# Diagonals of B written into zeros in DRAM and read back, in a four-layer selective-scan network

## The chip, the cores and the metric

The kernel runs on one core of a Trainium2 chip. A core has a matrix engine (TensorE, PE in the profile, its weight loads PEld), a vector engine (VectorE, DVE), an engine for activation functions and copies (ScalarE, ACT), a general engine (GpSimd, POOL) and a small one that here only issues DMA requests (SyncE, SP). Sixteen DMA engines move the data between DRAM and the on-chip memory. All arithmetic is in fp32. The metric is the time of one execution on the device, in microseconds (us); less is better. Times of single instructions come from one profiled execution.

## The reference

The input x has the shape 4 x 64 x 64 x 128. Layers 0, 1 and 3 are vision state-space blocks, layer 2 is a gated block that costs far less. A state-space block, cut to what matters here (DI = 256 channels, N = 16 states, R = 8, K = 4 directions, L = 4096 positions):

```python
xs    = stack([x0, x1, x0[..., ::-1], x1[..., ::-1]])      # rows, columns, both backwards
x_dbl = einsum('bkdl,kcd->bkcl', xs, x_proj_w)             # 8 + 16 + 16 rows: dt, B, C
delta = softplus(einsum('bkrl,kdr->bkdl', dts, dt_w) + dt_b)
h     = exp(delta_t * A) * h + (delta_t * x_t) * B_t       # for each position t, channel d and state n
y_t   = sum over n of h * C_t
```

In front of the scan stand a layer norm, a projection and a 3 x 3 depthwise convolution with SiLU; behind it a norm, a gate, a projection back and an MLP with GELU. The recurrence runs for 4 images x 3 layers x 4 directions x 256 channels x 16 states over 4096 positions.

## The kernel before

**Tiling.** The positions of one direction are cut into 8 chunks of 512. There are 12 turns (two images taken in turns through layers 0, 1 and 3), 32 chunks per turn (4 directions x 8), 384 chunks in all. Forward directions (k = 0, 1) make up 192 chunks, backward ones (k = 2, 3) the other 192. A chunk is worked through in eight periods, `i` = 0 to 7; a period handles 4 states (`CQ`) for one half of the channels (128 partitions). So period `i` uses the state group `q = i // 2`, and each group serves two periods.

**What a period does.** ACT computes the decays `exp(delta * A)` (`decay`, L907, tile `da`). DVE runs four scans over 512 positions (L923, tile `h`). The first two take their input `delta * x * B` from a PSUM tile `dbp`, which PE fills: `pair_db` (L898) multiplies the transposed `delta * x` (`duT`) with diagonal matrices that hold B for two states, so that the product is `delta * x` scaled by position. For the last two scans ACT copies `delta * x` (`du`) to PSUM (`lift`, L915, tile `dv`) and DVE multiplies it with rows of B spread over the partitions (L1050, L1051, tile `bb`). POOL multiplies the states with the spread rows of C (`times_c`, L935, tile `cb`; L937 adds in pairs in even periods). PE adds the products up into `yp` (`add_up`, L948). `dbp` has one buffer; `bb`, `cb`, `diag` and `xd` have two, `h` and `hc` four.

**The diagonals before.** `diagonals` (L884) makes, for one half of a state group, four 128 x 128 matrices on ACT, each the identity scaled by one column of `bt` (L890). `bt` is B with positions on the partitions: four transposes on PE (L850) and a copy on ACT (L855). One call stands at the end of each period, after `lift`; the two halves of a group are made three and two periods before the first period that scans with it.

**The prologue.** The rows [dt; B; C] of the next chunk are prepared meanwhile, piece by piece. `prologue` is a generator; `piece(2 * i)` in the middle of period `i` and `piece(2 * i + 1)` at its end advance it if the number is in `PIECES`. A forward chunk computes the rows of both directions (`ps_x`, L834), copies them to `xd` on ACT (L836), and stores them in DRAM (`xd_d`, L853), from where `spread` (L871) reads B and C back as broadcasts, one `bb` of 512 KB and one `cb` of 1 MB per state group, in odd periods, one group ahead. A backward chunk reads its rows from DRAM (L829). Before, the pieces are: 0 load of `xs`; 3 `xd` load or `ps_x`; 4 copy to `xd` and the first half of the dt product (L841); 6 and 8 delta (L844, L846) and the transposes of B; 9 the store of [dt; B; C], `bt` and the first `du`; 10 to 13 the rest.

**The order.** It is written out by hand: the instructions of each engine run in the order in which the Python code emits them, and each engine waits by semaphores. All DMA requests are issued by SP in that order, so one that must wait holds back all behind it. SP waits only for what a request needs, so it often stands periods ahead of the other engines. Between the steps of a period `other` slips in side work: the norms, projections, convolution and MLP that lead from one turn to the next (lines 190 to 759, tiles `gap`, `cen`, `wide`, `hid`). One of its requests is the store `x_col_d<-down` (L472), which writes a transposed image in runs of 8 values.

```python
    scan(s, i, 0, 1, da[0], s.db[:, :, 1])
    times_c(s, i, 0)
    if before:
        add_up(*before, 0)
    if then:
        pair_db(*then)          # dbp of the next period
    piece(2 * i)
    other(1)
    if spreads:
        spread(*spreads, 1)     # cb, in odd periods
```

Of the kernel before, what the change touches and what calls it, by code (L numbers as in the profile page):

```python
# [13 lines left out]
F32 = mybir.dt.float32  # L14
AF = mybir.ActivationFunctionType
# [7 lines left out]
DI, N, R, K = 256, 16, 8, 4  # L23
NX = R + 2 * N
HID = 4 * C
CH = 512
NCH = L // CH
RPC = CH // W
P = 128
WP = W + 2  # L30

CQ = 4

PAIRED = (0, 2, 4, 6)


PIECES = (0, 3, 4, 6, 8, 9, 10, 11, 12, 13)


_VSS = [  # L40
# [58 lines left out]
def vss_stack_kernel(ctx: ExitStack, tc: tile.TileContext, x: bass.AP, weights, out: bass.AP, n_batch=B, layers=(0, 1, 2, 3)):  # L99
# [6 lines left out]
    nc = tc.nc  # L106

    const = ctx.enter_context(tc.tile_pool(name="const", bufs=1))
    keep = ctx.enter_context(tc.tile_pool(name="keep", bufs=1, space=DRAM))

    ident = const.tile([P, P], F32, name="ident")
# [14 lines left out]
    for i in layers:  # L126
# [14 lines left out]
        t = const.tile([P, small_n + VSS_N - tail_at], F32, name=f"w{i}")  # L141
# [27 lines left out]
    def cols(c):  # L169
        return slice(c * CH, (c + 1) * CH)  # L170
# [13 lines left out]
    y_sb = const.tile([P, 2, L], F32, name="y_sb")  # L184
# [574 lines left out]
        return [S[a:z] for a, z in zip([0] + marks[1:], marks[1:] + [len(S)])]  # L759


    turns = []
    for e in range(0, n_batch, 2):
        for i in (0, 1, 3):
# [2 lines left out]
    for turn, (e, i) in enumerate(turns):  # L767

        for nth, k in enumerate((1, 3, 0, 2) if turn else (0, 1, 3, 2)):
            for ci in range(NCH):  # L770
                s = SimpleNamespace(turn=turn, e=e, v=wt[i], layer=i, nth=nth, k=k, ci=ci)
                s.c = NCH - 1 - ci if k >= 2 else ci
                s.columns, s.back = k % 2 == 1, k >= 2
                s.end = 0 if s.back else CH - 1
                s.step = slice(None, None, -1 if s.back else 1)
                s.first, s.last = ci == 0, ci == NCH - 1
                s.flip = len(chunks) % 2
                s.diag, s.cb, s.bb, s.h, s.hc = {}, {}, {}, {}, {}
                chunks.append(s)
    per_turn = K * NCH  # L780

# [27 lines left out]
    def scans(pool, ring, deep, psum):  # L809
# [4 lines left out]
        def prologue(s):  # L814


            lane, v = lanes[s.e % 2], s.v
            s.xs = ring.tile([P, 2, CH], F32, tag="xs", name="xs")
            nc.sync.dma_start(out=s.xs, in_=(lane.x_col if s.columns else lane.x_row)[:, :, cols(s.c)])
            if s.first:  # L820
                s.dt = pool.tile([R, DI], F32, tag="dt", name="dt_w")
                nc.sync.dma_start(out=s.dt, in_=weights[s.layer][1][:, s.k * DI : (s.k + 1) * DI])
            yield


            s.xd_d = lane.xd[s.k % 2][s.c]
            s.xd = pool.tile([2 * NX, CH], F32, tag="xd", name="xd")
            if s.back:
                nc.sync.dma_start(out=s.xd[:NX], in_=s.xd_d[1])  # L829
                yield  # L830
            else:
                ps = psum.tile([P, CH], F32, tag="misc", name="ps_x")
                for m in range(2):
                    nc.tensor.matmul(ps[: 2 * NX], v["xp"][:, s.k % 2, m, :], s.xs[:, m], start=(m == 0), stop=(m == 1))  # L834
                yield
                nc.scalar.copy(s.xd, ps[: 2 * NX])  # L836
            s.delta = pool.tile([P, 2, CH], F32, tag="delta", name="delta")
            halves = (s.flip, 1 - s.flip)
            for m in halves:
                ps = psum.tile([P, CH], F32, tag="misc", name="ps_dt")  # L840
                nc.tensor.matmul(ps, s.dt[:, m * P : (m + 1) * P], s.xd[:R], start=True, stop=True)  # L841
                yield
                func = AF.Identity if m == halves[0] else AF.Softplus
                nc.scalar.activation(s.delta[:, m], ps, func, bias=v["dtb"][:, s.k, m : m + 1])  # L844
            m = halves[0]
            nc.scalar.activation(s.delta[:, m], s.delta[:, m], AF.Softplus)  # L846
            nc.scalar.preload_act_table_set("natural_log_exp_and_others")
            ps = psum.tile([P, 4, NX], F32, tag="misc", name="ps_bt")
            for j in range(4):
                nc.tensor.transpose(ps[:, j, :], s.xd[:NX, j * P : (j + 1) * P], ident[:NX, :NX])  # L850
            yield
            if not s.back:
                nc.sync.dma_start(out=s.xd_d.rearrange("k r t -> (k r) t"), in_=s.xd)  # L853
            s.bt = pool.tile([P, 4, N], F32, tag="bt", name="bt")
            nc.scalar.copy(s.bt, ps[:, :, R : R + N])  # L855
            s.du = pool.tile([P, 2, CH], F32, tag="du", name="du")
            for m in halves:
                nc.gpsimd.tensor_mul(s.du[:, m], s.delta[:, m], s.xs[:, m])  # L858
                yield
            s.duT = pool.tile([P, 4, 2, P], F32, tag="duT", name="duT")  # L860
            for m in halves:
                ps = psum.tile([P, 4, P], F32, tag="misc", name="ps_duT")
                for j in range(4):
                    nc.tensor.transpose(ps[:, j, :], s.du[:, m, j * P : (j + 1) * P], ident)
                yield
                nc.scalar.copy(s.duT[:, :, m, :], ps)
            yield

        def spread(s, q, b):

            rows_of, at, count = ((s.bb, CQ * q + 2, CQ - 2), (s.cb, CQ * q, CQ))[b]  # L871
            rows_of[q] = pool.tile([P, count, CH], F32, tag="bc"[b] + "b", name="bc"[b] + "b")
            row = R + b * N + at
            nc.sync.dma_start(
                out=rows_of[q], in_=s.xd_d[s.k // 2 : s.k // 2 + 1, row : row + count].to_broadcast([P, count, CH])
            )
# [4 lines left out]
            q = i // 2  # L881
            return q, (i + q + s.flip) % 2

        def diagonals(s, q, half):  # L884

            if half == 0:
                s.diag[q] = pool.tile([P, 4, P, 2], F32, tag="diag", name="diag")
            for t in (2 * half, 2 * half + 1):
                for j in range(2):
                    nc.scalar.activation(  # L890
                        s.diag[q][:, t, :, j], ident, AF.Copy, scale=s.bt[:, t, CQ * q + j : CQ * q + j + 1]
                    )

        def pair_db(s, i):
            q, m = place(s, i)
# [6 lines left out]
        def decay(s, i, side):  # L902
            q, m = place(s, i)
            da = ring.tile([P, 2, CH], F32, tag="da", name="da")
            for j in range(2):
                n = CQ * q + 2 * side + j
                nc.scalar.activation(da[:, j], s.delta[:, m], AF.Exp, scale=s.v["a"][:, s.k, m, n : n + 1])  # L907
            return da
# [5 lines left out]
        def lift(s, i):  # L914
            nc.scalar.copy(dv[i % 2], s.du[:, place(s, i)[1]])  # L915
# [17 lines left out]
        def times_c(s, i, side):  # L933
            hc = s.hc[i, side] = deep.tile([P, 2, CH], F32, tag="hc", name="hc")
            nc.gpsimd.tensor_mul(hc, s.h[i, side], s.cb[i // 2][:, 2 * side : 2 * side + 2, :])  # L935
            if side == 1 and i in PAIRED:
                nc.gpsimd.tensor_add(hc, hc, s.hc[i, 0])  # L937

        def add_up(s, i, side):
            if side == 0 and i in PAIRED:  # L940
                return
            q, m = place(s, i)
            start, end = (0, 7) if m == s.flip else (1, 6)
            opens = i == start and side == int(i in PAIRED)
            if opens:
                setattr(s, f"yp{m}", psum.tile([P, CH], F32, tag=f"yp{m}", name="yp"))
            for j in range(2):
                nc.tensor.matmul(  # L948
                    getattr(s, f"yp{m}"),
                    ident,  # L950
                    s.hc[i, side][:, j],
                    start=opens and j == 0,
                    stop=i == end and side == 1 and j == 1,
                )
            if i == end and side == 1:
                full.append((s, m))
# [15 lines left out]
        for step in sum([combine(0, psums)] + opening[:4], []):  # L972
            step()
        s = chunks[0]
        pro = prologue(s)
        for _ in pro:
            pass
        for q, half in ((0, 0), (0, 1), (1, 0)):
            diagonals(s, q, half)
        spread(s, 0, 0)  # L980
        spread(s, 0, 1)
        pair_db(s, 0)
# [5 lines left out]
        for at, (s, i) in enumerate(periods):  # L988
            then = periods[at + 1] if at + 1 < len(periods) else None
            if i == 0:  # L990
                nxt = chunks[at // 8 + 1] if at // 8 + 1 < len(chunks) else None
# [14 lines left out]
            def piece(number):  # L1006

                if nxt and number in PIECES:
                    next(pro)
# [33 lines left out]
            other(1)  # L1043
            if spreads:
                spread(*spreads, 1)
            if then:
                da_next[1] = decay(*then, 1)
            save(s, i, 0)
# [6 lines left out]
            times_c(s, i, 1)  # L1055
            if then:
                lift(*then)

            q, half = (i + 2 + i % 2) // 2, 1 - i % 2
            if q < 4:  # L1060
                diagonals(s, q, half)
            elif nxt:
                diagonals(nxt, q - 4, half)
            if i < 2 and full:
                leave(*full.pop(0))
            if before:
# [108 lines left out]
```

## Time and profile before

| | |
|---|---|
| median of 3 runs | 22674.4 us (22664.0 to 22679.19) |
| the profiled execution's own time | 22684.1 us |
| its span, first to last instruction | 22682.3 us |
| granted TensorE clock, mean | 0.956 |
| busy: PE, DVE, ACT, POOL | 87%, 86%, 82%, 85% |
| DMA | 3060 MB in 2.44 million packets, 43.1% of 16 engines on SP's queue |
| first scan of turn 1, of turn 2 | 1982.3 us, 3791.2 us |

The profiled execution is 9.7 us above the median of the runs. Busy shares are shares of the span. A row of the groups reads: line, engine, operation, what is written from what, shapes and count; then busy us in total and mean ns of one; then the idle time of the engine ahead of them and what ended it. A row of the waits reads: who waited, for whom, us in total, times, and the longest. In the timeline a row has its start, its length, the engine (SPq is SP's request queue), the line and the tiles, and in brackets the idle time ahead of it. Turn 1 lasts from 1982.3 to 3791.2, 56.5 us per chunk; turn 3, which has the gated layer as its side work, from 5600.4 to 7587.3, 62.1 us per chunk.

### The profile page before, as it was taken

Reading aid. Unit: us, or ns where it says so; the run is one execution under the profiler, and the core shown is the slowest. Engines: PE = TensorE matmul, PEld = TensorE weight load, DVE = VectorE, ACT = ScalarE, POOL = GpSimd, SP = SyncE. Lnnn points to the kernel's source line nnn. Section 1 sums busy time; section 2 is a strip of 40 time slices with the busy share of each in tenths; the row PEclk is TensorE's granted clock in tenths of the full one; section 3 lists DMA queues with packets and bytes.
Section 4 is the critical chain, followed back from the end, with each engine's and each line's share of the span. In section 5 each row is a group of like instructions: output and inputs, shape, how many; then the busy total and the mean of one; then the engine's idle time right before and its main releaser. Section 6 shows DMA issues by size and latency. Waiting matters only on the chain. (4 is left out here: it accounts for less than half of the span.)

```text
span 22682.3 us, 216904 instructions
## 1 busy us (share of the span) xinstructions
PE 19815.6 (87%) x58234; PEld 10564.4 (47%) x58234; DVE 19497.9 (86%) x20186; ACT 18647.2 (82%) x40022; POOL 19246.5 (85%) x8862
## 2 busy tenths in 40 slices
PE   7888898888888888889889988888888888888887
PEld 3444444444444444444444444444444444444443
DVE  5999888988888888889889889898888888888996
ACT  5888888888887887888888888888888878888887
POOL 5999888888788878888888888888887888888996
PEclk8999999999999999999999999999999999999999
DMA  4444444444334434534534544444443453344333
GB/s 106 149 143 147 134 135 145 137 134 141 122 126 135 137 121 129 145 131 141 146 136 141 145 145 134 135 146 134 133 144 122 125 138 128 126 133 144 139 140 105
DMA packets 2437558, 3060.09 MB, mean 135 GB/s; under 512 B 1753840, under 2 KB 1790064, under 8 KB 2238192
## 3 DMA queue, kind: packets, MB, share of 16 engines
q1 hardware_dynamic: 2436336, 3046.22, 43.1%
q8 instruction: 472, 7.73, 0.1%
q14 instruction: 750, 6.14, 0.1%
HBM read 2784.41 MB, written 261.49 MB: 134 GB/s over the span
## 5 line engine op out<-in xcount | busy, mean ns | idle before, releaser
L935 POOL TENSOR_TENSOR hc<-h,cb 128x1024 f32<-128x1024 f32 x6144 | 14406.9, 2362 | 2937.3 <-DVE h L923 1825.8
L948 PE MATMUL yp<-hc,ident 128*128 128x512 f32 x18432 | 9030.4, 616 | 632.2 <-POOL hc L937 477.4
L907 ACT ACTIVATE da<-delta,w 128x512 f32<-128x512 f32 x12288 | 8149.8, 712 | 682.2 <-DVE h L923 668.0
L923 DVE TENSOR_TENSOR_SCAN h<-da,state,dbp 128x512 f32<-128x512 f32 x5376 | 6569.2, 1261 | 1123.5 <-PE dbp L898 893.0
L898 PE MATMUL dbp<-diag,duT 128*128 128x256 f32 x24576 | 6105.1, 392 | 1014.8 <-DVE h L923 965.7
L923 DVE TENSOR_TENSOR_SCAN h<-da,state,dv 128x512 f32<-128x512 f32 x5376 | 6583.5, 1263 | 0.0
L898 PEld LDWEIGHTS dbp<-diag,duT 128*128 128x128 f32 x24576 | 4720.4, 195 | 3320.5 <-issue 2038.1
L948 PEld LDWEIGHTS yp<-hc,ident 128*128 128x128 f32 x18432 | 3479.7, 196 | 4957.0 <-issue 3671.2
L890 ACT ACTIVATE diag<-ident,bt 128x128 f32<-128x128 f32 x12288 | 3951.5, 401 | 0.0
L937 POOL TENSOR_TENSOR hc<-hc 128x1024 f32<-128x1024 f32 x1536 | 3622.5, 2358 | 120.4
L915 ACT COPY dv<-du 128x512 f32<-128x512 f32 x3072 | 1800.2, 586 | 1208.3 <-DVE h L923 1202.0
L1050 DVE TENSOR_TENSOR dv<-dv,bb 128x512 f32<-128x512 f32 x3072 | 2083.0, 678 | 665.3 <-ACT dv L915 553.3
L1051 DVE TENSOR_TENSOR dv<-dv,bb 128x512 f32<-128x512 f32 x3072 | 2113.8, 688 | 0.0
L444 PE MATMUL gap<-halo,cw 128*128 128x512 f32 x3456 | 1757.2, 607 | 14.2 <-DVE cen L281 7.6
L841 PE MATMUL ps_dt<-xd,dt_w 8*128 8x512 f32 x1536 | 896.5, 664 | 287.1 <-DMA xd<-xd_d 149.8
L923 DVE TENSOR_TENSOR_SCAN h<-da,dbp 128x512 f32<-128x512 f32 x768 | 893.4, 1201 | 236.8 <-PE dbp L898 190.4
L858 POOL TENSOR_TENSOR du<-delta,xs 128x512 f32<-128x512 f32 x768 | 979.0, 1275 | 32.8 <-ACT delta L846 32.8
L931 ACT COPY state<-h 128x2 f32<-128x2 f32 x5376 | 962.1, 179 | 0.0
L444 PEld LDWEIGHTS gap<-halo,cw 128*128 128x128 f32 x3456 | 631.4, 192 | 661.9 <-issue 605.6
L923 DVE TENSOR_TENSOR_SCAN h<-da,dv 128x512 f32<-128x512 f32 x768 | 892.6, 1201 | 0.0
L844 ACT ACTIVATE delta<-ps_dt,w 128x512 f32<-128x512 f32 x768 | 524.5, 683 | 215.9 <-PE ps_dt L841 211.0
L281 DVE TENSOR_TENSOR cen<-cen,gap 128x512 f32<-128x512 f32 x256 | 175.0, 684 | 533.0 <-ACT gap L278 531.9
(122 smaller groups left out, 11908.7 us busy)
## 6 DMA issues: line engine op xcount, KB each, us to landing
cb<-xd_d SPq DMA_DIRECT2D x1536, 1024.0 KB
bb<-xd_d SPq DMA_DIRECT2D x1536, 512.0 KB
xs<-x_row_d SPq DMA_DIRECT2D x192, 512.0 KB
xs<-x_col_d SPq DMA_DIRECT2D x192, 512.0 KB
x_col_d<-down SPq DMA_DIRECT2D x192, 256.0 KB
x_row_d<-wide SPq DMA_DIRECT2D x96, 512.0 KB
y_d<-y_sb SPq DMA_DIRECT2D x96, 512.0 KB
y<-y_d SPq DMA_DIRECT2D x96, 512.0 KB
```

Of the source, the lines that this page charges most:

```text
L444: nc.tensor.matmul(z.ps, z.cw[:, m, t, :], z.halo[c][:, dy : dy + RPC, dx : dx + W], start=(t == 0), stop=(t == 8),)
L858: nc.gpsimd.tensor_mul(s.du[:, m], s.delta[:, m], s.xs[:, m])
L890: nc.scalar.activation(s.diag[q][:, t, :, j], ident, AF.Copy, scale=s.bt[:, t, CQ * q + j : CQ * q + j + 1])
L898: nc.tensor.matmul(s.db[:, t * P : (t + 1) * P, :], s.duT[:, t, m, :], s.diag[q][:, t], start=True, stop=True)
L907: nc.scalar.activation(da[:, j], s.delta[:, m], AF.Exp, scale=s.v["a"][:, s.k, m, n : n + 1])
L915: nc.scalar.copy(dv[i % 2], s.du[:, place(s, i)[1]])
L923: nc.vector.tensor_tensor_scan(s.h[i, side][:, j, s.step], da[:, j, s.step], db[:, s.step], init, ALU.mult, ALU.add)
L935: nc.gpsimd.tensor_mul(hc, s.h[i, side], s.cb[i // 2][:, 2 * side : 2 * side + 2, :])
L937: nc.gpsimd.tensor_add(hc, hc, s.hc[i, 0])
L948: nc.tensor.matmul(getattr(s, f"yp{m}"), ident, s.hc[i, side][:, j], start=opens and j == 0, stop=i == end and side == 1 and j == 1,)
L1050: nc.vector.tensor_mul(db, du, s.bb[i // 2][:, 0])
L1051: nc.vector.tensor_mul(du, du, s.bb[i // 2][:, 1])
```

## The change

The diagonals are no longer computed. Two DRAM arrays `diag_d`, one for even and one for odd chunks, are filled with zeros once at the start. Each has a part for each of the four state groups, of 512 rows of 258 values. For a chunk, two stores write 2048 single values each from `xd`: value t of B's rows for state j (0 or 1) of every group goes to place j of row t. Read with a row length of 256 instead of 258, row p of a block of 128 has these two values at 2p and 2p + 1, so a plain read of 512 KB gives the tile `diag` as `pair_db` wants it. The zeros around are never overwritten, and the values of the next chunk but one go to the same places.

The reads stand in odd periods right behind the request for C, one per odd period; the first `pair_db` that uses one is emitted two periods later. The transposes of B on PE and `bt` fall away. The store of [dt; B; C] moves from piece 9 to piece 5, with the two stores of values right behind it; the first half of the dt product moves from 4 to 5, its bias step from 6 to 7; the load of `xd` of a backward chunk moves from piece 3 to piece 0.

```diff
-PIECES = (0, 3, 4, 6, 8, 9, 10, 11, 12, 13)
+DIAG = 2 * P + 2
+PIECES = (0, 3, 4, 5, 7, 8, 9, 10, 11, 12, 13)
...
+    diag_d = []
+    zero = y_sb.rearrange("p m l -> p (m l)")[:, : N // CQ * 4 * DIAG]
+    nc.vector.memset(zero, 0.0)
+    for j in range(2):
+        diag_d.append(keep.tile([N // CQ, CH * DIAG], F32, name=f"diag_d{j}"))
+        nc.sync.dma_start(
+            out=diag_d[j].rearrange("q (p c) -> p q c", p=P), in_=zero.rearrange("p (q c) -> p q c", q=N // CQ)
+        )
...
+                s.diag_d = diag_d[s.flip]
...
-            yield
             s.xd_d = lane.xd[s.k % 2][s.c]
             s.xd = pool.tile([2 * NX, CH], F32, tag="xd", name="xd")
             if s.back:
                 nc.sync.dma_start(out=s.xd[:NX], in_=s.xd_d[1])
+            yield
+            if s.back:
                 yield
...
                 nc.scalar.copy(s.xd, ps[: 2 * NX])
+            yield
+            if not s.back:
+                nc.sync.dma_start(out=s.xd_d.rearrange("k r t -> (k r) t"), in_=s.xd)
+            rows = s.diag_d.rearrange("q (t c) -> q t c", c=DIAG)
+            for j in range(2):
+                nc.sync.dma_start(out=rows[:, :, j], in_=s.xd[R + j : R + N : CQ])
...
-            ps = psum.tile([P, 4, NX], F32, tag="misc", name="ps_bt")
-            for j in range(4):
-                nc.tensor.transpose(ps[:, j, :], s.xd[:NX, j * P : (j + 1) * P], ident[:NX, :NX])
             yield
-            if not s.back:
-                nc.sync.dma_start(out=s.xd_d.rearrange("k r t -> (k r) t"), in_=s.xd)
-            s.bt = pool.tile([P, 4, N], F32, tag="bt", name="bt")
-            nc.scalar.copy(s.bt, ps[:, :, R : R + N])
...
-        def diagonals(s, q, half):
-            if half == 0:
-                s.diag[q] = pool.tile([P, 4, P, 2], F32, tag="diag", name="diag")
-            for t in (2 * half, 2 * half + 1):
-                for j in range(2):
-                    nc.scalar.activation(
-                        s.diag[q][:, t, :, j], ident, AF.Copy, scale=s.bt[:, t, CQ * q + j : CQ * q + j + 1]
-                    )
+        def diagonals(s, q):
+            s.diag[q] = pool.tile([P, 4, P, 2], F32, tag="diag", name="diag")
+            nc.sync.dma_start(
+                out=s.diag[q].rearrange("p t c n -> p t (c n)"),
+                in_=s.diag_d[q].rearrange("(t p c) -> p t c", t=4, c=2 * P)[:P],
+            )
...
             if spreads:
                 spread(*spreads, 1)
+            if i % 2:
+                q = i // 2 + 2
+                if q < 4:
+                    diagonals(s, q)
+                elif nxt:
+                    diagonals(nxt, q - 4)
...
-            q, half = (i + 2 + i % 2) // 2, 1 - i % 2
-            if q < 4:
-                diagonals(s, q, half)
-            elif nxt:
-                diagonals(nxt, q - 4, half)
```

More of the change, by code (lines that the diff above doesn't have):

```diff
@@ L977, in scans @@
             pass
-        for q, half in ((0, 0), (0, 1), (1, 0)):
-            diagonals(s, q, half)
+        for q in range(2):
+            diagonals(s, q)
         spread(s, 0, 0)
@@ L1045, in scans @@
                 spread(*spreads, 1)
+            if i % 2:
+                q = i // 2 + 2
+                if q < 4:
+                    diagonals(s, q)
+                elif nxt:
+                    diagonals(nxt, q - 4)
             if then:
@@ L1057, in scans @@
                 lift(*then)
-            q, half = (i + 2 + i % 2) // 2, 1 - i % 2
-            if q < 4:
-                diagonals(s, q, half)
-            elif nxt:
-                diagonals(nxt, q - 4, half)
             if i < 2 and full:
```

## The prediction

> **What bounds the kernel now.** I read the page first, then the waits of each engine, then windows of single chunks, then the timeline. No engine is full:
>
> ```profile
> PE 19815.6 (87%) x58234; PEld 10564.4 (47%) x58234; DVE 19497.9 (86%) x20186; ACT 18647.2 (82%) x40022; POOL 19246.5 (85%) x8862
> ...
> L890 ACT ACTIVATE diag<-ident,bt 128x128 f32<-128x128 f32 x12288 | 3951.5, 401 | 0.0
> ```
>
> Four engines are within 5% of each other, so the loss lies in their waiting for one another. The second line is what the change takes off ACT: a fifth of its work, 32 instructions per chunk, 3951.5/384 = 10.3 us of a chunk's 59. What each chunk pays shows in windows laid on chunks (from one chunk's first scan to the next's); columns are the stretch, its length, busy us of PE, PEld, DVE, ACT, POOL, clock, DMA share, GB/s:
>
> ```profile
> 2492.60:2543.70 51.10, 50.50 (x156) 27.35 (x154) 49.73 (x52) 43.26 (x102) 47.52 (x22) 1.00 0.39 136
> ...
> 2605.30:2662.70 57.40, 50.61 (x150) 27.16 (x151) 51.16 (x54) 50.04 (x107) 50.79 (x23) 0.97 0.35 122
> 5928.50:5998.50 70.00, 57.41 (x164) 30.39 (x163) 54.47 (x58) 55.42 (x118) 52.02 (x24) 0.93 0.32 114
> ```
>
> Where ACT has 43 us of work the chunk lasts what PE is busy and no more (so does 3519.80:3570.50, with 41.6). Where side work (norms, MLP) brings ACT to 50 or 55, it lasts 7 to 13 us longer than PE is busy. The waits name the same engine:
>
> ```profile
> DVE h L923 <- PE dbp L898: 1083.4, 715, 14.5
> DVE dv L1050 <- ACT dv L915: 553.3, 276, 6.4
> DVE cen L281 <- ACT gap L278: 531.9, 206, 10.7
> ...
> DVE h L923 <- ACT diag L890: 36.8, 37, 3.1
> ```
>
> (total us, times, longest). DVE is idle for 22682 - 19498 = 3184 us, and the three rows on ACT with the two left out between them (y on gap 93.6 us in 58, h on da 65.2 in 46) hold 1281 us in 623 waits; the first row is PE's, and PE itself waits for ACT elsewhere. The timeline shows how such a wait comes about:
>
> ```profile
> 10010.47 2.07 PE L841 MATMUL ps_dt<-xd,dt_w 8*128 8x512 f32 x2 [5.17 <-ACT delta L844]
> ...
> 10012.15 0.70 DVE L1050 TENSOR_TENSOR dv<-dv,bb 128x512 f32<-128x512 f32 x1 [3.67 <-ACT dv L915]
> ```
>
> ACT has run late behind a gelu; PE stood 5.17 us, DVE 3.67 us, and each period puts another group of four diagonals, 1.28 us at 10012.05, into that queue.
>
> **What the change saves.** (1) ACT drops 4 instructions of 1.28 us together per period, and the 384 copies of bt. A wait on ACT is shortened by at least the one group ahead of it: 623 x 1.28 = 797 us. Bounds: 42 us (only the waits that name diag, 36.8 + 4.8) and 1281 us. I take 0.80 ms. (2) PE's rows that wait for ACT add up to 762 us of the 2867 us that PE is idle, 27%; that share of DVE's 1083 us on dbp is 0.29 ms (bounds 0 and 1083). The 1536 transposes of L850 (171 us busy) also go; I count nothing for them, since PE's idle time is larger. (3) For backward chunks xd is requested in step 0 instead of 3, one and a half periods earlier. The row "PE ps_dt L841 <- DMA xd<-xd_d: 149.8, 16" should vanish: 0.15 ms. Together 1.24 ms.
>
> **What it adds.** Per chunk there are four reads of 512 KB and two stores of 2048 single values, all on SP, which issues in order. The reads are 805 MB beside 3046 MB that take 43.1% of the DMA engines' time: by bytes 11% more. A diagonal is asked for right behind the C rows of one odd period and is first used by dbp two periods later, one period after those C rows; it needs half of their bytes, so C's lateness hides it. If C is on time and the diagonal is not, dbp and with it the next scan are late at once. It waits on SP for the dbp of the same period, which is emitted a period earlier; queued behind it are xs, the side work's loads and the next B rows, and these wait for later instructions anyway.
>
> The single values are the price. The nearest row is the x_col_d store, 8192 runs of 32 bytes. SP's next request behind it is held:
>
> ```profile
> 2367.46 0.37 SPq L472 DMA_DIRECT2D x_col_d<-down  x1
> 2367.88 4.51 SPq L477 DMA_DIRECT2D x_row_d<-wide  x1
> ...
> 2374.18 6.82 SPq L874 DMA_DIRECT2D cb<-xd_d  x1
> ...
> 2385.97 4.67 POOL L935 TENSOR_TENSOR hc<-h,cb 128x1024 f32<-128x1024 f32 x2 [10.00 <-DMA cb<-xd_d]
> ```
>
> A request takes 0.32 us as a rule, here 4.51 and 6.82 us, and POOL stood 10 us for a C that came 4.97 us after SP was done with it (2381.00 to 2385.97). That store takes 64 runs from each of 128 partitions, so each of 16 engines moves 512. The new store takes 512 from each of 4 partitions. If its values spread over all engines it holds SP for 2048/8192 x 4.51 = 1.13 us; if four engines share it, 512 each, for 4.51 us. I take 4.51, since a partition's values are more likely moved by one engine; both ends stay in the range. The Trainium skill, "DMA: Bandwidth & Descriptors", section "Why a DMA increments its semaphore by 16 and not by 1", says that a request uses the largest number up to 16 that divides the slowest dimension of both sides, which for 4 and 2048 is 4. By it the sum below stands; by the even spread it would be 0.46 ms better. The same page ("Issuing engines are not separate DMA queues") calls the issuing time usually small beside the transfer, which the 6.82 us above contradicts.
>
> In forward chunks the store can't go before ACT has copied xd. One such chunk (2209.4 to 2264.8), with the C of its periods 4 and 5; the B was asked for at 2221.04 and is first used by DVE at 2239.88:
>
> ```profile
> 2225.91 0.32 SPq L874 DMA_DIRECT2D cb<-xd_d  x1
> ...
> 2226.44 0.58 ACT L836 COPY xd<-ps_x 80x512 f32<-80x512 f32 x1
> ```
>
> After the change, these bb and cb stand behind the [dt; B; C] store (which before stood behind them) and both value stores. xd ends at 2227.0; +0.42 for its store, +0.37 for the first values, +4.51, +4.51: bb is through SP at 2236.8, cb at 2237.2, landed 4.97 us later at 2242.1 (bb, if it takes the 4.9 us of the store's case, at 2241.7, 1.8 us late; the two delays overlap). POOL takes that C as the third of the run that begins at 2235.07, at 2239.7: 2.4 us late. There are 192 forward chunks: 0.46 ms. In backward chunks xd comes by DMA, and the stores go out about a period earlier, with bb not yet free to be asked for: nothing. At the start a memset of 4128 columns (32 times the 0.17 us of the 128-column memsets) and 4.2 MB of zeros cost 0 to 25 us; I take 0.02 ms. The first dt matmul, its bias step and the [dt; B; C] store move by half a period to two periods with their consumers; nothing waits longer for them.
>
> **Sum.** 1.24 - 0.46 - 0.02 = 0.76 ms off the profiled execution's 22684.1 us (span 22682.3): 21924. The median of the runs is 9.7 us lower: 21915.
>
> **Rivals.** *The values are spread or absorbed.* Two holds of 1.13 us put cb at 2230.4, landed at 2235.4, nothing is late: 22674 - 1240 + 20 = 21455. For it speaks that DVE may run ahead of POOL by several tiles of h; against it the four source partitions.
>
> *The values are slow, and it ends slower.* A four-byte store into DRAM could cost more than a 32-byte run. The place is SP in period 2 of a forward chunk. The gain is gone at (1240 - 20)/192 = 6.35 us of lateness, that is at 4.51 + (6.35 - 2.4)/2 = 6.5 us per store, 12.7 ns per value with four engines. The 6.82 us above (a second store behind a first) shows that this is not far. At twice the 32-byte price, 9.0 us, C is 11.4 us late: 22674 - 1220 + 2190 = 23645. POOL would then show a long wait for cb in every forward chunk. With one engine alone it would be 27 ms, outside my range.
>
> *ACT is not what holds DVE.* PE waits for the scan to free dbp ("PE dbp L898 <- DVE h L923: 965.7, 697") and DVE for dbp: a ring without ACT. If it sets the pace, only 0.04 + 0.15 ms is saved against 0.48: 22965. The light chunks above, no longer than PE is busy, speak against it.
>
> **How the numbers follow.** Forecast 0.45, with its own range of 21460 (nothing late) to 22600 (second hold 6.8 us, nothing through PE); values spread or absorbed 0.13; slow values 0.24; no relief 0.18. About 0.2%, 45 us, is what a measurement here can tell from no change. The first two give faster, with a little from the last: 0.60. The edge between forecast and no relief gives 0.05 within 0.2%. Slower: 0.35. From 21200 (spread values with 0.25 ms more through PE) to 23500 (values at 1.9 times the 32-byte price) some 2 in 10 are left out, a little more of it above.
>
> **What would show it.** Right: ACT near 65% busy, no L890 group, the waits on ACT dv and gap halved, no wait for xd, light and heavy chunks closer together; SP held 4 to 5 us behind the value stores, and POOL waiting for cb more often, by 1 to 4 us, in forward chunks. Wrong: holds near 1 us, holds over 6.5 us, waits for diag at dbp, or DVE's waits moved whole from ACT to PE.

## The result and the profile after

The change makes the kernel slower. It takes 23585.5 us (median of 4 runs, 23570.5 to 23603.7) against 22671.0 us (22664.0 to 22679.2) for the kernel before, a ratio of 1.0404, 95% interval 1.0386 to 1.0422. That is 1.67 ms above the forecast, a little outside the range, and next to the rival "the values are slow, and it ends slower" (23645).

The page of the kernel after, busy times and DMA:

```profile
PE 19937.1 (85%) x56698; PEld 10630.6 (45%) x56698; DVE 19517.3 (83%) x20187; ACT 15289.8 (65%) x27350; POOL 19210.1 (82%) x8862
...
DMA packets 4825478, 3875.26 MB, mean 164 GB/s; under 512 B 3354384, under 2 KB 4177040, under 8 KB 4626192
```

ACT is at 65%, as forecast, and PE, DVE and POOL do about the work they did before. The span is 886 us longer all the same, so they wait more. The queue moves 27% more bytes but 98% more packets. The waits of DVE and POOL (total us, times, longest):

```profile
DVE dv L1069 <- DMA bb<-xd_d: 1296.6, 288, 17.3
DVE h L935 <- PE dbp L910: 1205.5, 830, 25.0
POOL hc L947 <- DMA cb<-xd_d: 1193.4, 177, 18.3
...
DVE cen L283 <- ACT gap L280: 433.9, 191, 10.6
...
DVE dv L1069 <- ACT dv L927: 258.5, 164, 4.6
```

The rows of the kernel before for the same two waits:

```profile
POOL hc L935 <- DMA cb<-xd_d: 550.4, 80, 14.3
...
DVE dv L1050 <- DMA bb<-xd_d: 105.2, 44, 7.1
```

The row of `bb` has grown twelvefold and now heads DVE's list. The waits for ACT were to halve: `dv` did (553.3 to 258.5), `gap` fell by a fifth only (531.9 to 433.9). The row on PE, `dbp`, grew (1083.4 to 1205.5). PE's waits for `xd` are gone.

The timeline of a forward chunk, the fifth of turn 1, shows the mechanism. Columns are start, length, engine or queue, line, tiles, and the idle time ahead with what ended it:

```profile
2330.17 0.58 ACT L852 COPY xd<-ps_x 80x512 f32<-80x512 f32 x1 [1.56 <-PE ps_x L850]
...
2330.78 0.32 SPq L855 DMA_DIRECT2D xd_d<-xd  x1
...
2331.15 5.12 SPq L858 DMA_DIRECT2D diag_d<-xd  x2
...
2336.36 5.88 SPq L889 DMA_DIRECT2D bb<-xd_d  x1
...
2342.34 0.38 SPq L889 DMA_DIRECT2D cb<-xd_d  x1
...
2347.63 0.70 DVE L1069 TENSOR_TENSOR dv<-dv,bb 128x512 f32<-128x512 f32 x1 [3.50 <-DMA bb<-xd_d]
...
2350.56 2.35 POOL L947 TENSOR_TENSOR hc<-h,cb 128x1024 f32<-128x1024 f32 x1 [6.84 <-DMA cb<-xd_d]
```

The second store of values is held behind the first, and `bb` behind the second for 5.88 us. `bb` is through SP at 2342.24 and lands 5.4 us later (2347.63); `cb` is through at 2342.72 and lands 7.8 us later (2350.56). By the trace's packets of 4 bytes the last of the chunk's 4096 values leaves at 2343.7. Before the change both requests stood ahead of the [dt; B; C] store, and each took about 0.3 us.

Worked out from the starts of all scans, the fifth period of a chunk (`i` = 4), where these B and C rows are first used, went from 7.75 to 10.42 us on average; no other period moved by more than 0.7 us.

### The profile page after: what moved, and what is told of

Its sections match the earlier page's. It is cut to its first block, busy times and chain, and to the rows that moved or that the text cites. A ratio compares the mean times of both kernels' runs of the same rounds, so it can differ in the third digit from the quotient of the medians.

```text
span 23568.8 us, 205065 instructions
## 1 busy us (share of the span) xinstructions
PE 19937.1 (85%) x56698; PEld 10630.6 (45%) x56698; DVE 19517.3 (83%) x20187; ACT 15289.8 (65%) x27350; POOL 19210.1 (82%) x8862
## 2 busy tenths in 40 slices
DMA packets 4825478, 3875.26 MB, mean 164 GB/s; under 512 B 3354384, under 2 KB 4177040, under 8 KB 4626192
## 5 line engine op out<-in xcount | busy, mean ns | idle before, releaser
L910 PE MATMUL dbp<-diag,duT 128*128 128x256 f32 x24576 | 6346.7, 405 | 1680.5 <-DVE h L935 816.0
L910 PEld LDWEIGHTS dbp<-diag,duT 128*128 128x128 f32 x24576 | 4872.6, 202 | 4085.1 <-issue 2918.1
L1069 DVE TENSOR_TENSOR dv<-dv,bb 128x512 f32<-128x512 f32 x3072 | 2089.5, 680 | 1625.8 <-DMA bb<-xd_d 1296.6
L881 ACT COPY duT<-ps_duT 128x512 f32<-128x512 f32 x768 | 448.1, 583 | 897.4 <-PE ps_duT L879 892.3
L446 PEld LDWEIGHTS gap<-halo,cw 128*128 128x128 f32 x3456 | 641.9, 192 | 549.3 <-issue 490.0
L863 PEld LDWEIGHTS ps_dt<-xd,dt_w 8*128 8x128 f32 x1536 | 230.3, 187 | 769.4 <-issue 355.6
```

Source lines behind the costliest of these rows:

```text
L446: nc.tensor.matmul(z.ps, z.cw[:, m, t, :], z.halo[c][:, dy : dy + RPC, dx : dx + W], start=(t == 0), stop=(t == 8),)
L910: nc.tensor.matmul(s.db[:, t * P : (t + 1) * P, :], s.duT[:, t, m, :], s.diag[q][:, t], start=True, stop=True)
L1069: nc.vector.tensor_mul(db, du, s.bb[i // 2][:, 0])
```

## The experiments

Two theories stood against each other for the missing gain and two for the loss. Gain: the waits on ACT come from its load (A), or from the chain of the step that waits, whatever ACT has to do (B). Loss: the stores of single values (S, called V in the expectation of e3), or the 805 MB of reads that share the DMA engines with everything else (R). All ratios are to the kernel before, run on the same chip, with 95% intervals.

**e1_before_no_diag: the relief of ACT alone.** In the kernel before:

```diff
+    diag_z = const.tile([P, 4, P, 2], F32, name="diag_z")
+    nc.vector.memset(diag_z, 0.0)
...
         def diagonals(s, q, half):
...
-                    nc.scalar.activation(
-                        s.diag[q][:, t, :, j], ident, AF.Copy, scale=s.bt[:, t, CQ * q + j : CQ * q + j + 1]
-                    )
+            s.diag[q] = diag_z
```

> The kernel before, with nothing for the diagonals: the 32 ACT instructions of a chunk are left out and dbp multiplies with one tile of zeros, so the first two states of each group get no input. All else stays, its order too. It measures what ACT's relief is worth by itself. Theory A (the relief is worth what the prediction said, 0.80 ms directly and 0.29 ms through PE): 21.6 ms, waits of DVE on ACT dv and gap halved. Theory B (ACT was one of four engines at the same load, and the other three still wait for one another): at most 0.3 ms, 22.4 to 22.7 ms, with ACT's idle time up by the whole 3.95 ms and ended by DVE.

Measured: 22379.4 us, 0.9869 (0.9853 to 0.9885). Taking all 12288 diagonals off ACT, with nothing in their place, saves 0.30 ms. Its waits:

```profile
DVE cen L283 <- ACT gap L280: 463.2, 196, 10.7
DVE dv L1046 <- ACT dv L911: 441.0, 227, 5.8
```

With `y` on `gap` (72.0 in 41) and `h` on `da` (31.9 in 41) the four rows on ACT hold 1008 us in 505 waits; with the row on `diag` (36.8 in 37), which is gone here, it was 1281 in 623. A wait still lasts 2.0 us on average (2.06 before); there are only some fewer. Windows laid on the same heavy chunk of turn 3 (its fifteenth) in the kernel before and in e1 (the columns are those of the windows above):

```profile
6502.10:6569.80 67.70, 53.81 (x156) 27.90 (x157) 54.20 (x60) 52.49 (x114) 52.70 (x25) 0.97 0.31 112
```
```profile
6419.80:6487.50 67.70, 53.83 (x156) 27.85 (x157) 54.21 (x61) 43.78 (x82) 52.48 (x25) 0.97 0.32 112
```

ACT has 8.7 us less to do and the chunk lasts 67.70 us in both. The timeline of e1 within that window shows one of its waits:

```profile
6439.33 0.63 ACT L271 ACTIVATE sq<-cen 128x512 f32<-128x512 f32 x1 [1.18 <-DVE cen L267]
...
6440.63 1.96 PE L894 MATMUL dbp<-diag_z,duT 128*128 128x256 f32 x8 [1.00 <-DVE h L919]
...
6442.53 1.12 PE L843 MATMUL ps_dt<-xd,dt_w 8*128 8x512 f32 x2
...
6443.58 1.13 PE L276 MATMUL gap<-sq,mean 128*128 128x512 f32 x2
...
6444.74 0.66 ACT L279 ACTIVATE gap<-gap,eps 128x512 f32<-128x512 f32 x1 [2.80 <-PE gap L276]
...
6445.44 0.58 ACT L280 ACTIVATE gap<-gap 128x512 f32<-128x512 f32 x1
6446.05 0.69 DVE L283 TENSOR_TENSOR cen<-cen,gap 128x512 f32<-128x512 f32 x1 [3.20 <-ACT gap L280]
```

The wait of `cen` is put down to ACT, but ACT itself had stood idle for 2.80 us: the square is done at 6439.96, its mean on PE stands in order behind a `dbp` that waits for DVE's own scan, and then two short steps on ACT follow. The kernel before has the same 2.80 and 3.20 us in the same place (ACT at 6527.07, DVE at 6528.38). There the row on ACT is the last hop of a chain.

Over all waits the picture is mixed. Worked out from the trace of e1, such chains make up much of the row on `gap`: in 111 of its 196 waits ACT was idle for a part, 146 us of 463 in all. In the waits on `dv`, however, ACT worked for 437.8 of the 441.0 us: on decays, copies, loads of its function tables and side work. There DVE does wait behind ACT's queue, but in the kernel before the diagonals were little of what ACT did meanwhile: 26 of the 553 us of the row on `dv`, and 139 of the 1281 us of all five rows, in which it was busy for 1108. So the relief is worth what theory B allowed, and far from the 1.09 ms of A; B's chains are shown for `gap` alone. Why one group of diagonals less per period shortened the waits on `dv` by so little (112 us in all, net) stays open.

**e2_after_no_dma and e3_after_no_values: which of the DMAs costs.** In the kernel after, e3 leaves out the two stores and keeps the reads; e2 leaves out the reads as well.

```diff
 # e2 and e3
-            rows = s.diag_d.rearrange("q (t c) -> q t c", c=DIAG)
-            for j in range(2):
-                nc.sync.dma_start(out=rows[:, :, j], in_=s.xd[R + j : R + N : CQ])
 # e2 alone
+            s.diag[q] = diag_z
-            s.diag[q] = pool.tile([P, 4, P, 2], F32, tag="diag", name="diag")
-            nc.sync.dma_start(out=s.diag[q]..., in_=s.diag_d[q]...)
```

> The changed kernel without its new DMA traffic: neither the two stores of values nor the four reads of diagonals; dbp multiplies with a tile of zeros. The new places of the [dt; B; C] store and of the xd load stay. Theory A: 21.4 to 21.6 ms (relief 1.09 ms, earlier xd 0.15 ms). Theory B: like e1, less 0.15 ms for xd, 22.3 to 22.5 ms. If moving the [dt; B; C] store ahead of B and C were itself the loss, this one would be slower than e1.

> The changed kernel without the two stores of values; the four reads of 512 KB stay and bring zeros. Theory V (the stores are the whole loss): within 0.1 ms of e2, and 1 to 2 ms under the changed kernel's 23.59 ms; B and C in period 4 of forward chunks are on time. Theory R (805 MB of reads delay B and C by themselves): 0.5 ms or more above e2, with waits of POOL for cb spread over all periods.

Measured: e2 22377.9 us, 0.9868 (0.9853 to 0.9883); e3 22330.5 us, 0.9848 (0.9833 to 0.9863). With the reads the kernel isn't slower than without them (though PE waits 208.1 us for diagonals in e3), and both stand where e1 stands. So the reads cost no time that shows, the new places of the prologue's steps are worth 0.05 ms at most, and the two stores cost 23585.5 - 22330.5 = 1255 us: theory S. The waits of e3 for the spread rows are those of the kernel before again:

```profile
POOL hc L944 <- DMA cb<-xd_d: 519.3, 78, 12.9
...
DVE dv L1066 <- DMA bb<-xd_d: 130.7, 46, 6.4
```

Worked out from the first scans of the chunks, one in which the values of a forward chunk are stored takes 57.73 us in e3 and 62.26 after, 4.53 us more; with those of a backward chunk 57.23 and 59.10, 1.87 us more. Times 192 each, this is 1229 of the 1255 us. TensorE's granted clock falls too, from 0.958 in e3 to 0.941, and PE is busy 331 us longer with the same 56698 instructions; how much of the loss passes through this no run separates.

The packets hint at how many engines a store used. After has 4825478 - 3249534 = 1575944 packets more than e3, 384 x 4104 but for 8: two stores of 2048 values and 4 further packets each, taken here as end packets.

**e4_split8: the same values over more engines.** Each store is cut into four, one for each state group:

```diff
-                nc.sync.dma_start(out=rows[:, :, j], in_=s.xd[R + j : R + N : CQ])
+                for q in range(N // CQ):
+                    nc.sync.dma_start(out=rows[q : q + 1, :, j], in_=s.xd[R + j + CQ * q : R + j + CQ * q + 1])
```

> The changed kernel with each store of 2048 values split into four stores of 512 values, one partition each; the same values go to the same places. If a store of four partitions runs on four of the sixteen DMA engines and one of a single partition of 512 values is spread over sixteen, SP is held by each of the eight requests for under 1 us, 3 to 5 us in all instead of 11, B and C come 6 to 8 us earlier, and the time is e3 plus 0.1 to 0.4 ms. If the time per value is what counts and not the number of engines, SP is held for 11 us as before and the time stays at 23.5 ms; if a single partition goes to one engine, 24 ms and more.

Measured: 22979.4 us, 1.0133 (1.0118 to 1.0149). The packets grow by 46100, 384 x 120 but for 20: eight stores with 16 end packets each in place of two with 4. Read as one end packet per engine, the stores of the change ran on four engines each and these on sixteen. That agrees with the rule of the Trainium skill that the prediction cites from "DMA: Bandwidth & Descriptors", section "Why a DMA increments its semaphore by 16 and not by 1". Of the loss of 1255 us about half goes (22979.4 is 649 us above e3). The eight requests of a chunk still take long on SP, with `bb` and `cb` behind them:

```profile
2326.92 7.84 SPq L859 DMA_DIRECT2D diag_d<-xd  x8
```

That is 7.84 us for 4096 values with sixteen engines to a store, each store reading one partition. By the packets a chunk's values take 9.3 us to leave here (median of the chunks), against 11.3 us after the change, so sixteen engines move single values little faster than four. DVE waits 667.5 us for `bb`, POOL 784.6 us for `cb`.

**e7_one_store: is the cost in proportion?** Only the first of the two stores is left.

```diff
-            for j in range(2):
+            for j in range(1):
```

> The changed kernel with one of its two stores of values; the second state of each group gets no input. Theory H: lateness has a threshold. With one store SP is through some 6 us earlier, C comes at about the time at which POOL wants it, and only a quarter or less of the 1.26 ms between e3 and the changed kernel is left: 22.4 to 22.65 ms. Theory L: half of it, 22.96 ms.

Measured: 22487.6 us, 0.9915 (0.9901 to 0.9930). Half of the values cost 157 of the 1255 us. This fits a reserve that the delay eats first: with one store POOL waits 687.4 us for `cb` and DVE 272.5 us for `bb`, with two 1193.4 and 1296.6. By the trace's packets the two stores of the change leave at some 340 values per us after a faster start, 11.3 us for a chunk's 4096 (about 11 ns per value on each of four engines); one store takes half of that, and B and C then come nearly on time.

**e5_values_behind_c: another place for the stores.** They stand behind the request for C in period 3, ahead of the read of a diagonal.

```diff
 # in the period's order
             if spreads:
                 spread(*spreads, 1)
+            if i == 3 and nxt:
+                values(nxt)                 # the two stores, taken out of prologue
             if i % 2:
                 q = i // 2 + 2
```

> The changed kernel with one move: the two stores of values are issued in period 3 behind the request for C and ahead of the diagonal's, instead of in period 2 ahead of B and C. Theory H (the loss is that B and C of period 4 stand on SP behind two stores that hold it for 5 to 6 us each): B and C are on time again and the time falls to e3 plus 0.1 to 0.4 ms, 22.4 to 22.7 ms; what remains is the B request of period 5, asked for 2 us later at most. Theory L (4096 single values load the DMA engines and the loss follows their number, wherever they stand): 23.3 to 23.6 ms as before.

Measured: 22887.6 us, 1.0095 (1.0078 to 1.0112). B and C are on time (DVE waits 143.4 us for `bb`, POOL 549.3 us for `cb`), and yet it is slower than before: the request behind the stores is now a diagonal. From the timeline and the waits of e5:

```profile
2279.48 9.31 SPq L899 DMA_DIRECT2D diag_d<-xd  x2
...
2288.89 5.89 SPq L903 DMA_DIRECT2D diag<-diag_d  x1
```
```profile
PE dbp L912 <- DMA diag<-diag_d: 896.4, 205, 18.3
```

The values take the same 11.3 us to leave as after the change (median of the chunks in both), but they start later, while the bytes of C still move: SP is held for 9.31 + 5.89 = 15.2 us here, against 5.12 + 5.88 = 11.0 us in the chunk shown above. The delay is no smaller and has changed its victim; the period that ends with the first use of this diagonal (`i` = 5) went from 6.60 us in e3 to 8.10.

**e6_bt_values: fewer, wider runs from 128 partitions.** B is transposed on PE as before the change, four small copies bring the eight columns that are needed into `bt`, and one store writes 2048 runs of two values.

```diff
-            rows = s.diag_d.rearrange("q (t c) -> q t c", c=DIAG)
-            for j in range(2):
-                nc.sync.dma_start(out=rows[:, :, j], in_=s.xd[R + j : R + N : CQ])
+            ps = psum.tile([P, 4, NX], F32, tag="misc", name="ps_bt")
+            for j in range(4):
+                nc.tensor.transpose(ps[:, j, :], s.xd[:NX, j * P : (j + 1) * P], ident[:NX, :NX])
+            yield
+            s.bt = pool.tile([P, 4, 4, 2], F32, tag="bt", name="bt")
+            for q in range(4):
+                nc.scalar.copy(s.bt[:, q], ps[:, :, R + CQ * q : R + CQ * q + 2])
+            places = s.diag_d.rearrange("q (t p c) -> p q t c", t=4, c=DIAG)
+            nc.sync.dma_start(out=places[:, :, :, :2], in_=s.bt)
```

> The values go out from 128 partitions: the four transposes of B on PE come back, four small ACT copies put the two values of each group side by side in a tile bt of 128 x 32, and one store of 2048 runs of 8 bytes takes the place of two stores of 2048 runs of 4. The diagonals are read as in the changed kernel, its places kept, the store one piece later. If the x_col_d store is the price (8192 runs over sixteen engines hold SP 4.5 us), SP is held for 2048/8192 x 4.5 = 1.1 us, nothing is late and the time is that of e3 within 0.15 ms: 22.3 to 22.5 ms, faster than the kernel before. If runs of 8 bytes cost what they cost from four partitions (11 ns each on four engines in a row), 5.6 us: 22.6 to 23.0 ms.

Measured: 22739.6 us, 1.0028 (1.0017 to 1.0038), a miss. The store is cheap now. As with the stores of the change, its price shows at the request behind it, which takes 0.87 us by the median (0.32 us as a rule, 5.9 us behind the two stores), and its 2048 runs leave in 1.5 us. But it has a new wait, and that wait stands ahead of `cb`:

```profile
2295.49 0.37 SPq L864 DMA_DIRECT2D diag_d<-bt  x1
2295.95 0.87 SPq L895 DMA_DIRECT2D cb<-xd_d  x1
```
```profile
SPq L864 <- ACT bt L862: 3119.0, 361, 18.7
```
```profile
POOL hc L953 <- DMA cb<-xd_d: 1350.0, 341, 15.7
```

**e8_plain_columns: does the older store of many runs cost too?** In the kernel before, `x_col_d` is written as one run per partition, not 64.

```diff
-                to_col = lane.x_col[:, m].rearrange("p (w h) -> p w h", h=H)
-                nc.sync.dma_start(out=to_col[:, :, c * RPC : (c + 1) * RPC], in_=z.down)
+                nc.sync.dma_start(out=lane.x_col[:, m, cols(c)], in_=z.down.rearrange("p w h -> p (w h)"))
```

> The kernel before with the x_col_d store as one run of 2 KB per partition instead of 64 runs of 32 bytes; the column image is therefore not transposed. It asks whether a store of many short runs costs the kernel before as well. Theory H: SP is no longer held for 4.5 and 7 us behind each of the 192 stores, POOL's 550 us of waiting for C shrink to under 200, and the time falls by 0.2 to 0.4 ms, to 22.3 to 22.5 ms. Theory L: the stores are 8% of the DMA time and hidden: 22.65 ms or more.

Measured: 22108.1 us, 0.9750 (0.9735 to 0.9764). It does, by 0.57 ms: POOL's wait for `cb` falls from 550.4 to 115.3 us and DVE's for `bb` from 105.2 to 3.4. Nearly all lateness of the spread rows in the kernel before comes from these stores.

**e9_bt_behind_diag and e10_values_behind_diag: cheap or late.** Both put the stores behind the read of the diagonals in period 3, where nothing due soon follows; e9 takes e6's store from `bt`, e10 the two stores of the change.

```diff
                 elif nxt:
                     diagonals(nxt, q - 4)
+            if i == 3 and nxt:
+                values(nxt)
```

> The kernel after with the values stored from 128 partitions (B transposed on PE, four small copies to bt, one store of 2048 runs of 8 bytes), as in e6_bt_values, but the request for that store stands behind the read of the diagonals in period 3, so that neither B, C nor a diagonal of that period waits behind it. The whole result is computed. Theory S (the loss is the place and the price of the stores on SP): nothing due soon stands behind the store, the wait of SP for bt harms nobody, and the time comes near that of the kernel without any value stores, 22330: 22350 to 22500, faster than the kernel before (22675) by about 1%. Theory W (moving B's transposes and copies into the prologue's steps 5 and 6 costs by itself): it stays near e6_bt_values, 22650 to 22750, with POOL's waits for cb back at about 550.

> The kernel after with its two slow stores of 2048 single values each unchanged, but placed behind the read of the diagonals in period 3, where only the loads of the side work and, in period 5, the next B, C and diagonal stand behind them. Whole result computed. Theory S: they take about 11.3 us to drain and there are some 14 us to the next due requests; the wait for diag that e5_values_behind_c showed (896 us) goes back to some 200 and the time is 22350 to 22550. Theory D (the drain of 4096 values disturbs other transfers wherever it stands): B, C of period 5 and the diagonal behind them come late, 22700 to 22900.

Measured: e9 22438.7 us, 0.9888 (0.9873 to 0.9903); e10 22569.9 us, 0.9947 (0.9935 to 0.9960). Both compute the whole result and beat both kernels. Waits of e9, then of e10:

```profile
POOL hc L955 <- DMA cb<-xd_d: 584.7, 91, 12.6
...
PE dbp L918 <- DMA diag<-diag_d: 201.4, 38, 10.7
...
DVE dv L1080 <- DMA bb<-xd_d: 135.2, 48, 7.3
```
```profile
POOL hc L949 <- DMA cb<-xd_d: 664.0, 112, 18.0
...
DVE dv L1074 <- DMA bb<-xd_d: 329.0, 91, 14.3
```

In e9 all three stand near e3. In e10 the slow stores still reach some B and C rows, and the time is just above what theory S gave. So the same values, the same reads and the same relief of ACT are worth +4.0% or -0.5% by the place of two requests alone. e9 stays about 0.4% above e3; DVE's wait on `dbp` is 106 us longer there (1257.6 against 1151.1 us), with the transposes back on PE, but no run separates that. e1 to e3 multiply by zeros for half of the states; e9 works on all of them at a granted clock of 0.960 (0.958 in e3), so the zeros can be no more than a small part of what e3 gains.

## Why the prediction was wrong

The prediction had the right two effects and mis-sized both, by 0.90 ms on the gain and 0.80 ms on the loss; together this is the miss of 1.67 ms.

- **Saving (1), 0.80 ms, is the step that failed first.** "A wait on ACT is shortened by at least the one group ahead of it" multiplied 623 waits by 1.28 us. e1 takes every group away, and the waits on ACT lose 273 us and the kernel 0.30 ms. The step took an engine that is named last for one that the diagonals make late. The trace of before had a warning: in those 1281 us ACT was idle for 173 (as in the 2.80 us that it waited for PE), worked on diagonals for 139, and on other things for the rest. The case that I showed, where ACT had run late behind a gelu, is of the kind that the row on `dv` is full of; but what it is late with there is mostly side work, table loads and decays.
- **Saving (2), 0.29 ms through PE, was nothing:** the `dbp` row is 1078.9 us in e1, 1083.4 before. Saving (3), 0.15 ms for the earlier `xd`: the wait went, the time did not; e3 is 49 us below e1, with overlapping intervals. Together 0.30 to 0.34 ms in place of 1.24.
- **The rival "ACT is not what holds DVE" was right on the gain.** I spoke against it with the light chunks, which last no longer than PE is busy, and so took ACT for what makes heavy chunks long. What a heavy chunk has more of is side work, with chains through PE, ACT and DVE as in the one shown. Light and heavy chunks were to come closer together; the sixth chunk of turn 3, 70.00 us long before with 55.42 us of ACT, has 45.44 us of ACT after the change and lasts 72.10 us, with the delay of the stores in it. Without them it is 68.8 us in e3, and 67.8 us in e1.

- **The cost, 0.46 ms, is 1.255 ms.** Its mechanism was right: the place on SP, four engines to a store, a first hold of about 5 us (5.3 by the median of all chunks), `bb` and `cb` late together. Three terms were too small. The second store's hold was taken as 4.51 us and is 5.88. The landing after SP was taken as 4.9 and 4.97 us, from another case, and is 5.4 and 7.8: in the chunk shown, values still leave for 1.5 us after `bb` is through SP, and the packets of C come behind those of B. And backward chunks were costed at "nothing", because their stores were to go out a period earlier. They don't always: in this one the stores are issued behind a side-work request, with the same hold on `bb`:

```profile
2784.70 0.37 SPq L577 DMA_DIRECT2D xn_d<-halo  x1
2785.16 5.50 SPq L858 DMA_DIRECT2D diag_d<-xd  x2
2790.72 5.92 SPq L889 DMA_DIRECT2D bb<-xd_d  x1
```

  4.53 us for forward and 1.87 us for backward chunks stand where I had 2.4 and 0. That the second half of the values costs seven times the first, e7's result, is how a modest error of the holds could become a large one of the sum.
- **The sign hung on the gain.** The prediction's own 0.46 ms of cost against the measured 0.34 ms of gain already ends slower. The break-even that it gives, 6.5 us per store, used 1.24 ms of gain; with 0.34 ms it lies at 1.8 us of lateness per forward chunk, below its own 2.4. The upper end of the forecast's own range, 22600, is a slip of the sum: its terms add up to about 22650.
- **What held:** the reads hidden (e3 against e2); four engines per store (the packets); ACT at 65%; the start, where the first scan comes 19.8 us later (0.02 ms).

## What to carry to other kernels

A row of waits names the engine that came last, not one that is overloaded: before costing its relief, see what that engine did during those waits, and count the part that is the work to be taken away (139 of 1281 us here). The bytes of a store did not tell its price here (16 KB took 11.3 us to leave as single values from four partitions, and 1.5 us as runs of two from 128), and the requests behind it in the queue paid: list those with the time at which each is due, and give the store the place behind which nothing is due soon. When such a store is moved or made cheaper, look for the next victim and for the new wait that it brings (a diagonal in e5, the wait for `bt` in e6).

## What the runs showed of the hardware

Writing single 4-byte values from four partitions took about 2.8 us per thousand values with four DMA engines by the end packets (4096 in 11.3 us). Spread over sixteen engines, one partition per store, they still held SP for 7.84 us and took 9.3 us to leave: the number of engines was not the only limit there, and no run shows what the other is. The same values as 2048 runs of 8 bytes from 128 partitions left in 1.5 us, and the request behind them took 0.87 us. The long-standing `x_col_d` stores of 8192 runs each, which I had used only as a yardstick, cost the kernel before 0.57 ms, nearly twice what all diagonals on ACT do.
